# A written-out order of 3,830 pieces, replaced by another order of the same pieces

## The chip, the cores and the metric

The kernel runs on one core of a Trainium2 chip. The metric is the device time of one execution in microseconds. The core has five instruction queues that run side by side: TensorE (PE, with its weight loads PEld), VectorE (DVE), ScalarE (ACT), GpSimd (POOL) and SyncE (SP), which here issues the DMAs. Each queue runs its instructions in the order in which the program issued them; an instruction waits on semaphores for what it needs from other queues, and everything behind it on its own queue waits with it.

## The reference

32 sequences of 256 tokens with 128 channels go through one block: a layer norm and a Mamba (selective state space) layer with a residual, then a layer norm and a mixture of 8 experts, of which the router takes 2 for each token.

```python
xi, res = split(layernorm(x) @ W_in)            # 256 inner channels each
u  = silu(causal_conv4(xi) + conv_b)
dt, B, C = split(u @ W_x)                       # rank 8, 16 states, 16 states
delta = softplus(dt @ W_dt + b_dt)
h[t] = exp(delta * A) * h[t-1] + delta * u * B  # for each channel and state
y = sum_n(h * C) + u * D
x = x + (y * silu(res)) @ W_out
scores = layernorm(x) @ gate_w.T                # the best two, softmax, weights cw
x = x + sum_e cw[e] * (silu(layernorm(x) @ w1[e].T) @ w2[e].T)
```

The kernel computes all 8 experts for every token and weighs them with `cw`, which is zero for six of them.

## The kernel before

The sequences are cut into 17 tiles: tiles 0 and 16 hold one sequence, tiles 1 to 15 two. One tile goes through some 230 pieces. A piece is a small function that issues one or a few instructions, mostly to one engine. A long string, `ORDER`, lists all 3,830 pieces of all tiles as `tile:piece`, and the kernel runs through it once:

```python
    with tc.manual_schedule():
        for word in ORDER.split():
            i, n = word.split(":")
            pieces[n](int(i))
```

So the string alone sets the order within each engine's queue, and with it which buffer is given out when. No scheduler comes after it. Its words interleave about three tiles at a time: while one tile's scans run, the experts of the tile before and the convolution of the tile after stand between them. The pieces, in the order that one tile needs them, with their lines:

- Start: `ldx` (load x, SP), `st1`, `sa1` (statistics and their aggregation for the layer norm, DVE, L538 and L544), `rs1` (four small POOL instructions, L554 to L557), `ap1` (normalise, ACT, L563), `tr1`, `hi1`, `nl1`, `lo1` (transpose on PE and split into a high and a low part, PE and ACT alternately).
- Convolution: `cv0`, `cv1` (12 matmuls each, PE, L635), `u0`, `u1` (silu, ACT, L649). Gate: `gp`, `gs` (PE L703, ACT silu L718).
- State-space inputs: `wx` (PE, L658), `sb`, `rh`, `nr`, `rl` (ACT and PE), `bcd` (rows B and C to DRAM, SP), `rb`, `rc` (B and C rows broadcast to 128 partitions, SP, L778), `zz` (PE), `sp` (softplus, ACT, L739), `du` (POOL, L793), `dp` (copy of du to PSUM, ACT, L799).
- Scans, 16 for a tile of two sequences and 8 for a tile of one, 256 in all: `dk` (decays, ACT exp, L760), `in` (product du times B row into the one PSUM tile `db`, DVE, L818), `sc` (scan, DVE, L825), `cm` (weigh with the C row, POOL, L836; once `cn`, on DVE, L840), `ys` (transposing sum onto y, PE, L844; L862 for the first of a half).
- After a half of the scans: `yc` (copy y, ACT), `yz` (times gate, POOL, L924; once `yv`, on DVE), `yt` (transpose, PE), `ye` (copy, ACT, L944). Then `ldr` (x again, SP), `px` (residual, PE, L956), `op` (output matmul, PE, L966), `x2` (copy, ACT), and `st2`, `sa2`, `rs2`, `ap2`, `tr2`, `hi2`, `nl2`, `lo2` as above.
- Router: `gt` (PE), `sc` without a number (two reductions, DVE, L1052), `r0` to `r3` (DVE, L1059 to L1079), `r4`, `rw0`, `rw4`, `rw3` (POOL), `rx` (exp, ACT), `rw1`, `rw2` (DVE).
- Experts: for each of 8, `wi` twice (PE, L1125), `si` twice (silu, ACT, L1138), `wo` (16 matmuls, PE, L1146), `as` (scale by cw, ACT, L1158) and `aa` (add, POOL, L1164), or in part of the last two tiles `ad` (DVE, L1169); at the end `sto` (store, SP).

Constants are loaded and prepared by pieces of tile 0 (`lw`, `lc`, `l1`, `ld2`, `km`, `kh`, `kl`, `kw`, `pm`, `kdg`, `kgt` and others), also placed by the string.

Buffers bind the queues to one another: 9 tiles `da` of decays, 4 each of B and C rows, 3 of scan results h, one `db`, one `du`, two of x, 2 of `so` and 4 working tiles in PSUM. A scan with number k of its tile needs the h buffer that the `ys` of three scans before has freed. The B rows of four and the C rows of three scans in the middle of a tile are kept for its second half, which runs the states in the opposite order.

ACT's functions lie in three tables (exp, silu, softplus). `need()`, L530, issues a table load whenever the next function is in another table than the last one, so the number of loads follows from the order too.

Of the kernel before, what the change touches and what calls it, by code (L numbers as in the profile page):

```python
# [47 lines left out]
0:pm 0:ldx 0:lw0 0:lw1 0:lc0 0:lc1 1:ldx 0:ldp 0:st10 0:st11 0:sa1 0:rs1 0:ap1 0:km1 0:tr1 0:kh1 0:hi1 0:nl1  # L48
0:km0 0:kh0 0:lo1 0:kl1 1:st10 1:st11 1:st13 1:st12 0:kl0 0:kwr 0:cv1 0:cv0 1:sa1 1:rs1 3:ldx 3:st10 0:ldd
0:ldk 0:ka 0:u1 1:ap1 1:tr1 0:u0 0:wx 0:gp0 0:sb 0:rh 0:kdt 1:hi1 0:nr 0:rl 0:gs0 1:nl1 0:zz 0:pb0 1:lo1 0:sp0  # L50
0:pc0 0:l11 0:ldg 0:ld2 0:l10 2:ldx 2:st10 3:st13 0:kw0 0:kw1 2:st12 0:dq0 2:st11 2:st13 0:in0 2:sa1 0:bcd
0:rc0 0:rc3 0:rb1 0:rc1 0:rb2 0:dk0 0:dk2 0:dk1 0:sc0 0:cm0 0:in1 0:sc1 0:in2 0:kgt 0:sc2 0:dk5 0:dk3 2:rs1
2:ap1 0:kdg 0:cm1 1:gp0 1:cv1 1:cv0 1:u0 0:ys0 1:u1 0:dk4 0:ys1 1:wx 1:rh 1:sb 0:dk6 0:dk7 0:rb3 0:in3 0:dq1
0:sc3 0:in4 0:sc4 0:in6 0:rc7 0:rc2 0:cm2 0:cm3 0:ys2 1:nr 1:rl 0:sc6 1:bcd 0:ldr 0:ys3 1:zz 1:sp0 0:yc0 1:sp1
0:in5 3:st11 0:sc5 1:rb1 1:rb5 0:cm4 0:ys4 1:rc0 1:rb4 0:ldo 0:yz0 0:yt0 0:cm6 1:rc3 1:du0 0:cm5 0:ys5 0:px
0:ys6 0:in7 1:rb0 0:sc7 0:cm7 0:ys7 1:gp1 1:gs0 2:tr1 1:dk5 1:dp0 1:in1 1:rb6 4:ldx 3:st12 1:dk1 1:sc1 1:in0
1:dk0 1:dk3 0:ye0 1:dk8 1:dk2 0:yc1 0:yz1 2:hi1 1:rb2 1:rc1 1:sc0 1:cm0 3:sa1 0:yt1 2:nl1 0:ye1 0:op 0:st20
1:dk6 2:lo1 2:gp0 0:st21 0:sa2 0:rs2 1:cm1 1:in2 1:ys0 1:rc2 1:rb3 0:x2 1:gs1 0:ap2 0:tr2 0:hi2 1:sc2 1:in5
4:st10 1:sc5 0:nl2 0:lo2 2:gs0 0:wi50 0:gt 1:ys1 0:sc 1:in3 1:rc5 1:rc13 0:r3 1:sc3 1:cm2 1:rc4 1:rb7 0:pt
0:r4 1:cm3 1:du1 1:rc7 0:si50 1:dk9 1:dk11 1:dk4 0:rx 1:dk10 1:dk12 1:in4 2:cv1 1:ys2 0:r0 1:sc4 1:cm4 1:rc6  # L60
1:cm5 1:in6 0:r1 0:wi40 2:cv0 1:ys3 1:sc6 0:si40 0:wi70 2:u1 0:wi51 2:u0 0:wi00 0:si70 0:si51 1:in7 0:r2 2:wx
1:ys4 1:ys5 0:wi20 0:wi41 3:rs1 1:cm6 0:rw0 0:rw4 1:dk7 1:sc7 1:cm7 0:si00 0:wi21 2:rh 0:si20 0:wi60 1:dp1
1:in8 4:st13 2:sb 2:bcd 1:rb15 2:nr 0:si21 2:gp1 0:si60 0:wi01 0:si01 3:ap1 1:sc8 0:wi10 0:si10 0:si41 1:ys6
0:wi30 0:si30 2:gs1 2:rl 1:ys7 2:zz 0:wo0 3:tr1 1:in9 1:rb13 1:ldr 0:rw1 1:cm8 1:sc9 1:in10 1:rb12 0:rw2
1:sc10 0:rw3 1:in11 4:st12 1:rc11 2:rb3 2:sp0 0:wo4 2:sp1 1:yc0 3:hi1 1:ys8 1:sc11 1:in12 0:wi11 0:as4 0:wo2
0:as0 0:wi71 3:nl1 0:si11 1:dk13 3:lo1 2:dk3 1:cm9 1:rc12 1:rb14 1:ys9 1:cm10 1:ys10 3:cv0 1:yz0 0:aa4 0:as2
0:si71 1:dk15 1:dk14 1:cm11 1:ys11 0:wi61 1:rc15 4:st11 1:sc12 1:in13 2:rb0 1:rc14 4:sa1 1:sc13 1:in14 2:rb4
1:sc14 0:wo7 0:wi31 1:in15 0:aa2 0:as7 2:du0 1:cm12 2:rc0 1:ys12 1:yt0 1:cm13 0:aa0 2:du1 1:cm14 2:rb1 1:sc15
1:cm15 2:rc2 2:dk6 2:dk0 3:u0 3:gp1 1:ys13 1:ys14 1:ys15 0:si61 0:si31 2:dp0 2:in0 2:rb5 2:rc1 2:sc0 2:in1
2:rb2 2:dk7 2:dk1 2:sc1 2:in3 2:dk2 1:yc1 2:dk4 1:ye0 2:dk8 2:dk5 2:sc3 2:in2 3:cv1 3:gp0 1:px 2:rc3 2:cm0  # L70
2:ys0 2:sc2 3:u1 1:yz1 1:yt1 2:cm1 2:cm3 2:cm2 1:ye1 1:op 2:ys1 1:st20 2:in4 3:gs0 3:gs1 2:dk9 2:dk11 2:dk10
# [12 lines left out]
2:op 3:ys0 2:st20 4:tr1 3:in3 2:st21 2:st22 3:sc3 2:st23 3:in4 2:sa2 1:as4 1:wo2 3:ys1 3:sc4 3:dk7 1:as5 1:aa5
3:cm2 2:rs2 3:dk11 3:dk10 4:hi1 4:nl1 1:wo7 3:ys2 1:as2 4:lo1 2:x2 3:dk12 2:ap2 4:cv0 3:rb5 3:in5 5:sa1 3:sc5
3:rc5 3:rb7 3:rb6 3:rc4 3:rc6 2:tr2 4:u0 3:in6 6:st10 2:hi2 3:cm3 4:gp0 2:nl2 3:ys3 4:cv1 4:gs0 2:lo2 3:dk9
3:sc6 1:aa2 1:as7 3:dk13 3:cm4 5:rs1 3:du1 3:cm5 3:in7 3:dp1 3:dk15 6:st13 3:ys4 3:sc7 3:cm6 3:rc12 3:rc7 2:gt
2:sc 3:in8 2:r0 3:rb13 3:ys5 2:wi00 4:gp1 2:si00 2:wi30 4:u1 4:wx 4:gs1 2:wi60 3:ys6 3:sc8 3:cm7 5:ap1 2:si60
2:si30 4:sb 2:r1 3:in9 2:r3 3:sc9 3:ys7 2:wi20 2:si20 4:rh 2:wi70 2:wi61 4:nr 2:si70 3:yc0 4:rl 2:si61 3:dk14
3:in10 2:r2 3:sc10 2:wi50 3:cm8 3:ys8 3:cm9 3:ys9 4:zz 2:wi21 1:aa4 2:r4 2:rx 2:rw0 3:ldr 3:rc13 3:rb12 4:bcd  # L90
3:rc11 4:rb1 3:in11 4:sp0 2:wi71 4:sp1 2:wi31 2:si21 2:si31 2:si71 2:rw4 2:rw1 3:sc11 3:in12 3:cm10 3:ys10
2:wi01 5:tr1 2:wi40 2:si01 2:si50 2:si40 2:wi10 2:si10 5:hi1 2:wi41 2:wi51 2:rw2 3:sc12 4:du0 1:aa7 3:cm11
3:cm12 2:rw3 3:yz0 3:rb14 3:rc15 3:in13 3:rb15 3:rc14 4:rb4 3:sc13 3:in14 3:cm13 4:rb0 2:wi11 2:si11 2:si51
2:si41 3:ys11 2:wo2 2:wo3 3:ys12 5:nl1 3:yt0 3:sc14 4:rc0 4:rc1 3:cm14 4:dk3 4:dk2 2:as3 2:as2 2:aa3 3:ys13
2:wo1 3:ys14 2:wo0 3:in15 4:dp0 6:st11 4:rb3 3:sc15 4:in0 6:st12 3:cm15 4:rb2 2:aa2 3:ys15 4:dk0 4:sc0 4:cm0
# [12 lines left out]
4:in15 7:st11 4:rc14 4:cm14 5:rb4 4:rc15 5:rb0 5:rb3 5:dp0 6:lo1 5:dk7 4:ys13 3:aa1 3:wo5 4:ys14 3:wo0 5:dk4
3:as5 3:as2 4:sc15 4:cm15 3:aa5 4:ys15 3:wo4 4:yc1 3:as0 4:yz1 5:dk2 5:in1 5:rc0 5:rb2 7:st12 5:sc1 5:in0
# [1162 lines left out]
```

## Time and profile before

| | us |
|---|---|
| Median of 3 runs (lowest, highest) | 1044.05 (1043.04, 1046.95) |
| The profiled execution | 1043.46 |
| Its span, first to last instruction | 1041.7 |
| POOL weighing `cm` L836, 255 instructions | 604.2 busy, 2.38 each |
| DVE scan L825, 256 | 584.3 busy, 2.28 each |
| DVE product L818, 256 | 314.9 busy, 1.23 each |
| ACT decays L760, 544 | 341.1 busy |
| ACT table loads L530, 105 | 134.7 busy, 1.28 each |
| PE sums `ys` L844, 2,048 matmuls | 268.8 busy |
| PE expert matmuls L1125 and L1146 | 215.8 and 249.1 busy |
| Landing of a C row (median), 205 loads of 512 KB | 5.1 |
| Landing of a B row (median), 187 loads of 512 KB | 4.8 |

The span is what lies between the first and the last instruction. An engine's busy time leaves out its waits. A wait is named by the engine that waits and the work that released it. Matmuls are pipelined, so a mean duration of a matmul is longer than its share of PE's time.

### The profile page before, as it was taken

To read this page: it belongs to the slowest core of one execution; us is meant where nothing else is said; L and a number is where in the kernel's file an instruction comes from. 1 tells how busy PE (TensorE), PEld (TensorE's weight loads), DVE (VectorE), ACT (ScalarE), POOL (GpSimd) and SP (SyncE) were. 2 spreads that over 40 slices of the span, in tenths; PEclk is the share of its full clock that TensorE was granted. 3 is DMA by queue.
4 is the path that set the end of the run, shared out by engine and by line. 5 is a ranking of instruction groups with operands and counts; after the bars stand their busy time and mean duration, and the time that the engine had idled before them with its cause. 6 is when DMAs were issued, how large, how long until landed. Compare 5 with 4: busy or idle time off the path is not lost.

```text
span 1041.7 us, 18833 instructions
## 1 busy us (share of the span) xinstructions
PE 952.9 (91%) x6693; PEld 833.6 (80%) x6693; DVE 967.1 (93%) x946; ACT 944.7 (91%) x1893; POOL 901.8 (87%) x676
## 2 busy tenths in 40 slices
PE   6578789899999999999999999999989999899998
PEld 5467678879798888879888887888878788787888
DVE  4999999999999999999999999999999999999963
ACT  6889989989899999989999898989979999899975
POOL 2668888999899999998899999998989999899962
PEclk9789999999999999999999999999999999999999
DMA  7474848668476776847586685858668585865500
GB/s 234 155 258 161 284 167 274 219 215 284 172 256 189 254 257 205 282 157 260 197 266 240 209 268 174 273 175 277 222 196 272 179 279 178 269 232 197 182 11 16
DMA packets 86094, 223.75 MB, mean 215 GB/s; under 512 B 8048, under 2 KB 35312, under 8 KB 85872
## 3 DMA queue, kind: packets, MB, share of 16 engines
q1 hardware_dynamic: 86000, 222.55, 64.5%
q8 instruction: 52, 0.85, 0.3%
q14 instruction: 42, 0.34, 0.1%
HBM read 217.28 MB, written 5.24 MB: 214 GB/s over the span
## 4 chain that ended last, share of the span: by engine, by line
PE 31%; ACT 26%; DVE 21%; POOL 15%; issue 6%; DMA 1%; SPq 0%; DVEq 0%; POOLq 0%; ACTq 0%
DVE h L825 13%; ACT da L760 9%; PE pf L1125 9%; POOL h L836 9%; PE pe L1146 7%; DVE db L818 6%; PE y L844 6%; ACT L530 5%; POOL x L1164 3%; ACT so L1158 3%; PE pc L635 3%; ACT hs L1138 2%; PE po L966 1%; PE pd L658 1%; ACT xn_c L563 1%
## 5 line engine op out<-in xcount | busy, mean ns | idle before, releaser
L836 POOL TENSOR_TENSOR h<-h,rc 128x1024 f32<-128x1024 f32 x255 | 604.2, 2379 | 67.4 <-DVE h L825 56.3
L825 DVE TENSOR_TENSOR_SCAN h<-da,db 128x1024 f32<-128x1024 f32 x256 | 584.3, 2282 | 21.9 <-PE y L844 7.6
L760 ACT ACTIVATE da<-de,a_sb 128x510 f32<-128x510 f32 (+1 forms) x544 | 341.1, 718 | 0.9 <-DVE h L825 0.5
L818 DVE TENSOR_TENSOR db<-du,rb 128x1024 f32<-128x1024 f32 x256 | 314.9, 1230 | 11.2 <-ACT du L799 2.1
L844 PE MATMUL y<-ident,h 128*128 128x128 f32 x2048 | 268.8, 278 | 20.0 <-POOL h L836 19.5
L844 PEld LDWEIGHTS y<-ident,h 128*128 128x128 f32 x2048 | 237.2, 144 | 39.2 <-POOL h L836 26.7
L1146 PE MATMUL pe<-w_sb,hs 128*128 128x128 f32 x2048 | 249.1, 276 | 3.8 <-ACT so L1158 2.8
L1146 PEld LDWEIGHTS pe<-w_sb,hs 128*128 128x128 f32 x2048 | 238.8, 192 | 11.3 <-ACT so L1158 4.4
L1125 PE MATMUL pf<-xt,w_r 128*128 128x512 f32 (+1 forms) x816 | 215.8, 399 | 12.5 <-ACT hs L1138 7.3
L1138 ACT ACTIVATE hs<-pf 128x512 f32<-128x512 f32 (+1 forms) x272 | 144.6, 577 | 40.3 <-PE pf L1125 36.6
L1125 PEld LDWEIGHTS pf<-xt,w_r 128*128 128x128 f32 x816 | 138.6, 189 | 52.9 <-ACT hs L1138 19.7
L1164 POOL TENSOR_TENSOR x<-x,so 128x512 f32<-128x512 f32 (+1 forms) x126 | 157.5, 1250 | 10.5 <-ACT so L1158 9.2
L1158 ACT ACTIVATE so<-pe,cw 128x128 f32<-128x128 f32 x488 | 140.4, 393 | 6.4 <-PE pe L1146 4.1
L530 ACT ACT_TABLE_LOAD x105 | 134.7, 1283 | 1.9
L635 PE MATMUL pc<-xt_r,wc_r 128*128 128x512 f32 (+1 forms) x408 | 99.9, 396 | 1.1 <-ACT xt_r L624 1.1
L635 PEld LDWEIGHTS pc<-xt_r,wc_r 128*128 128x128 f32 x408 | 73.8, 197 | 15.4 <-issue 0.8
L862 PE MATMUL y<-dg_sb,u 128*128 128x128 f32 x256 | 36.4, 285 | 11.7 <-ACT yt L917 6.9
L862 PEld LDWEIGHTS y<-dg_sb,u 128*128 128x128 f32 x256 | 32.6, 195 | 17.0 <-ACT yt L917 10.6
L924 POOL TENSOR_TENSOR g<-yt,g 128x512 f32<-128x512 f32 (+1 forms) x33 | 40.7, 1233 | 5.6 <-ACT yt L917 2.9
L793 POOL TENSOR_TENSOR dus<-de,u 128x512 f32<-128x512 f32 (+1 forms) x32 | 39.8, 1247 | 0.0
L966 PE MATMUL po<-wo_sb,yt 128*128 128x128 f32 x256 | 32.8, 277 | 2.3 <-ACT yt L944 2.2
L966 PEld LDWEIGHTS po<-wo_sb,yt 128*128 128x128 f32 x256 | 30.8, 192 | 4.9 <-ACT yt L944 3.2
(101 smaller groups left out, 716.8 us busy)
## 6 DMA issues: line engine op xcount, KB each, us to landing
rc<-bc SPq DMA_DIRECT2D x205, 512.0 KB, 5.1
rb<-bc SPq DMA_DIRECT2D x187, 512.0 KB, 4.8
xa<-in_x SPq DMA_DIRECT2D x15, 256.0 KB, 4.4
xc<-in_x SPq DMA_DIRECT2D x15, 256.0 KB, 4.4
out<-x SPq DMA_DIRECT2D x15, 256.0 KB, 6.0
w1h<-in_w_t SPq DMA_DIRECT2D x2, 512.0 KB, 7.1
w_sb<-in_w_t SPq DMA_DIRECT2D x1, 1024.0 KB, 7.6
bc<-s SPq DMA_DIRECT2D x32, 32.0 KB, 3.1
```

What stands on the lines that cost most here:

```text
L530: nc.scalar.preload_act_table_set(SETS[which])
L635: nc.tensor.matmul(pcv, wc_r[a][:, j, c * P : (c + 1) * P], xt1_r[b][:, : nb[i], o + j : o + j + L], start=(k == 0), stop=(k == 3 * KC - 1),)
L760: nc.scalar.activation(da[:, m, :, 1:], de[:, :, 1:], AF.Exp, scale=a_sb[:, c, n : n + 1])
L818: nc.vector.tensor_mul(db, d["du"].unsqueeze(1).to_broadcast([P, gs[i], tok[i]]), rows["b", i, k])
L825: nc.vector.tensor_tensor_scan(flat(h), da_of(i, k), flat(d["db"]), 0.0, ALU.mult, ALU.add,)
L836: nc.gpsimd.tensor_tensor(h, h, rows["c", i, k], ALU.mult)
L844: nc.tensor.matmul(y[:, q, :], src[:, q * P : (q + 1) * P], ident, is_transpose=True, start=False, stop=last, skip_group_check=True,)
L1125: nc.tensor.matmul(pf, w1_r[a][:, e, f * P : (f + 1) * P], d["xt"][b], start=(k == 0), stop=(k == 2),)
L1138: nc.scalar.activation(d["hs", e][:, f, :], d["pf", e, f], AF.Silu)
L1146: nc.tensor.matmul(pe[:, q, :], hs[:, f, q * P : (q + 1) * P], w2_sb[:, e, f, :], start=(f == 0), stop=(f == FC - 1),)
L1158: nc.scalar.activation(so[:, q, :], d["pe", e][:, q, :], AF.Copy, scale=d["cw"][:, q, e : e + 1])
L1164: nc.gpsimd.tensor_tensor(x2, x2, st[i]["so", e], ALU.add)
```

## The change

Nothing but the string `ORDER` is replaced, on lines 47 to 284. Both strings hold the same 3,830 words. 3,627 of them stand at another place; a word is moved by 10.1 places on average and by 187 at most, and the longest run of words that keep their order among themselves has 1,769. The arithmetic, the buffers and the number of instructions that the pieces issue stay as they are. The number of table loads that follows from the order is 105 before (106 with the first one, L563) and 106 after (107).

The first lines of both, and the words from the last scan on:

```diff
-0:pm 0:ldx 0:lw0 0:lw1 0:lc0 0:lc1 1:ldx 0:ldp 0:st10 0:st11 0:sa1 0:rs1 0:ap1 0:km1 0:tr1 0:kh1 0:hi1 0:nl1
-0:km0 0:kh0 0:lo1 0:kl1 1:st10 1:st11 1:st13 1:st12 0:kl0 0:kwr 0:cv1 0:cv0 1:sa1 1:rs1 3:ldx 3:st10 0:ldd
-0:ldk 0:ka 0:u1 1:ap1 1:tr1 0:u0 0:wx 0:gp0 0:sb 0:rh 0:kdt 1:hi1 0:nr 0:rl 0:gs0 1:nl1 0:zz 0:pb0 1:lo1 0:sp0
...
-16:sc7 16:cn7 15:rw1 15:rw2 15:rw3 16:yz0 14:aa4 14:sto 15:wo5 16:px 15:wo1 16:ys5 16:ys6 15:si01 16:yt0 16:ys7
-16:yv1 15:as1 15:wi21 16:ye0 16:yt1 15:as5 15:wi61 16:ye1 16:op 16:st20 16:st21 16:sa2 16:x2 15:si61 15:si21
...
+0:ldx 0:lw0 0:lc0 0:lc1 0:ldg 1:ldx 0:ldk 0:ldd 0:ldp 0:l11 0:lw1 0:l10 0:ld2 0:st10 0:st11 0:sa1 0:pm 0:rs1
+0:ap1 3:ldx 0:km1 0:tr1 0:kh1 0:hi1 0:nl1 0:lo1 1:st10 1:st13 1:st12 0:kl1 0:cv1 1:st11 1:sa1 1:rs1 0:kdg 0:km0
+0:ka 0:kh0 1:ap1 2:ldx 0:u1 0:kwr 0:kl0 0:cv0 1:tr1 0:u0 0:wx 0:gp0 0:rh 0:sb 1:hi1 0:nr 0:rl 0:gs0 0:kdt 0:zz
...
+16:sc7 15:rw1 16:cn7 16:ys7 16:yt0 15:wi21 16:yv1 15:wo1 15:rw2 15:rw3 15:as5 15:si21 16:ye0 16:px 16:yt1 15:wi61
+16:ye1 15:as1 15:si61 15:aa1 16:op 16:st20 16:st21 16:sa2 16:x2 16:rs2 15:wo0 15:as0 16:ap2 15:wo3 15:wi71 16:tr2
```

The line breaks are set anew here. ACT's decays from the end of tile 13 to the start of tile 14, in the order in which they are issued (other words between them left out):

```diff
-13:dk10 13:dk8 13:dk11 13:dk9 13:dk12 13:dk15 13:dk13 13:dk14 14:dk0 14:dk1 14:dk2 14:dk3 14:dk4 14:dk5 14:dk6
+13:dk12 13:dk8 13:dk11 13:dk10 13:dk9 13:dk15 13:dk13 13:dk14 14:dk0 14:dk3 14:dk1 14:dk4 14:dk5 14:dk2 14:dk6
```

## The prediction

> **What bounds the kernel now.** I read the page first, then busy time by stretches, then the waits, then VectorE's own timeline. The page and the stretches:
>
> ```profile
> span 1041.7 us, 18833 instructions
> PE 952.9 (91%) x6693; PEld 833.6 (80%) x6693; DVE 967.1 (93%) x946; ACT 944.7 (91%) x1893; POOL 901.8 (87%) x676
> ...
> 0.00:60.00 60.00, 35.35 (x162) 29.03 (x163) 45.87 (x58) 47.52 (x88) 28.75 (x46) 0.83 0.59 199
> 190.00:320.00 130.00, 125.35 (x906) 111.10 (x904) 125.73 (x124) 123.55 (x248) 120.88 (x88) 1.00 0.69 227
> 960.00:1042.00 82.00, 76.09 (x599) 71.08 (x597) 52.56 (x78) 61.27 (x152) 51.83 (x45) 1.00 0.23 81
> ```
>
> The columns of a stretch are its length and the busy time of PE, PE's weight loads, DVE, ACT and POOL. In the middle four engines are busy over 90% of the time and DVE most, 125.73 of 130. At the end PE leads and DVE has little left. So the middle is VectorE's, and the end TensorE's.
>
> ```profile
> 122.22 1.23 DVE L818 TENSOR_TENSOR db<-du,rb 128x1024 f32<-128x1024 f32 x1
> 123.59 2.29 DVE L825 TENSOR_TENSOR_SCAN h<-da,db 128x1024 f32<-128x1024 f32 x1
> 125.91 1.23 DVE L818 TENSOR_TENSOR db<-du,rb 128x1024 f32<-128x1024 f32 x1
> 127.28 2.29 DVE L825 TENSOR_TENSOR_SCAN h<-da,db 128x1024 f32<-128x1024 f32 x1
> ...
> 235.56 1.23 DVE L818 TENSOR_TENSOR db<-du,rb 128x1024 f32<-128x1024 f32 x1
> 236.70 0.28 DVE L538 BATCH_NORM_STATS2 st_a<-xa 128x6 f32<-128x128 f32 x1
> 236.92 2.29 DVE L825 TENSOR_TENSOR_SCAN h<-da,db 128x1024 f32<-128x1024 f32 x1
> ```
>
> This is VectorE's timeline (start, duration). With nothing else between, scan follows scan after 3.69 us (127.28 - 123.59), and product to scan takes 1.37. With a 0.28 us statistic between product and scan it takes 1.36 (236.92 - 235.56): the small piece runs in a gap that is there anyway.
>
> That lets me write the span as a sum. The first scan starts at 25.92 and the last at 1002.96. Between them lie 255 intervals; 255 x 3.69 = 941.0, and 1002.96 - 25.92 = 977.0, so 36.1 us are lost in the middle. In VectorE's timeline the idle times in brackets between these two scans add up to 16.7 us (36 waits, none over 1.2); the other 19.4 are small pieces that found no gap. Head 25.9 + 941.0 + 36.1 + end 38.7 = 1041.7. The profiled execution took 1043.46, 1.8 more than its span, and the median is 1044.05, 0.6 above that; I subtract from the median.
>
> ```profile
> DVE h L825 <- PE y L844: 7.6, 14, 1.2
> POOL h L836 <- DVE h L825: 56.3, 46, 13.5
> POOL h L836 <- DMA rc<-bc: 5.8, 3, 4.6
> ```
>
> The waits (total, times, longest): the scan mostly waits for the transposing sums `ys`, which free one of the three h buffers. The rest of the 16.7 is ACT's du copy 2.1, router scores from PE 1.8, `po` 1.5, decays `da` 1.3 and single cases.
>
> **The change, part by part.** No instruction is added or taken away but one activation-table load. Every saving must come from the head, the 36.1 or the end.
>
> *The 941.0 stays:* the same 256 scans and products, both orders with one product in each interval.
>
> *Small pieces on VectorE.* I sorted the 255 intervals by what the order puts between two scans, and before (pre) or after (mid) the product, and priced each pattern by its undisturbed intervals in the timeline, as the excess over 3.69: one statistic mid 0.02, four aggregates mid 0.06, `r0` mid 0.11, `st in st` 0.05, `st in st st` 0.25, `r0 in r1` 0.29, `r1 in r2` 0.29. The old order then costs 20.5 (19.4 by the subtraction above), the new one 18.5. The difference, 2.0, is mostly these: `st in st st` goes from 6 intervals to 0 (-1.5) while `st in st` goes from 3 to 10 (+0.4), `r0 in r1` from 4 to 2 (-0.6) while `r1 in r2` goes from 4 to 6 (+0.6), and two long router and statistics clusters, of tiles 16 and 1, lose 0.3 each. I take -2.0; bounds -3 and 0.
>
> The Trainium skill ("VectorE: DVE Perf Modes", section "The DRAIN you can't avoid") says that the next op starts only when the pipe is empty, and advises to minimize the number of ops. By that rule a small piece costs the same wherever it stands, and this term would be 0. The rows above speak against it: 0.28 us of statistic between product and scan cost nothing.
>
> *Waits of VectorE, 16.7.* What makes `ys` late is other work crowded in front of it on PE, or POOL's weighing `cm` behind other work. h has three buffers, so I looked at three scans at a time: the row times of all that stands in an engine's queue between one `ys` (or `cm`) and the third after it, less 3 x 3.77 (3.77 is 977.0 less 16.7, over 255). Row times are 0.9 for a `ys`, 1.8 for a `wo`, 0.75 for a `wi`, 2.8 for a `cv`, 2.38 for a `cm`, 1.28 for an `aa`. On PE the worst stretch exceeds by 10.5 in the old order and by 7.5 in the new; over all stretches the excess is about the same (+3%). On POOL the worst falls from 8.2 to 6.7, the sum by 21%. A wait arises only where a stretch outruns the buffers, so I go by the worst ones: 7.5 / 10.5 = 0.71, and 16.7 x 0.71 = 11.9, or -4.8. Bounds: -16.7 (all gone) and +16.7 (an equal amount of new ones, since nearly every queue is reshuffled).
>
> *Loads on SP.* I counted for each row load how many scans lie between the one that frees its buffer and the one that needs it. C rows with a lead of one scan: 3 in the old order, 0 in the new; leads of two: 19 and 17; B rows are as before (1 and 1, 35 and 36). Their cover is the lead: two scans are 7.4 us, against a median landing of 5.1. POOL waited only 5.8 us for such rows, and VectorE hardly felt it, so 0; without that cover a late C row costs up to the 4.6 of its longest wait. `ldr` moves forward by 26 places on average, past row loads; it needs a freed x buffer, and a blocked SP would delay the rows behind it. I keep that inside the +16.7.
>
> *The table load.* The order alternates exp, silu and softplus 105 times before, 106 times now. One load is 1.28 us of ACT, which in the middle idles 6.4 of 130 us, and its lead over VectorE covers it: 0. Uncovered it costs 1.3, since ACT's queue then delays a decay and VectorE's next scan.
>
> ```profile
> 961.56 1.28 ACT L530 ACT_TABLE_LOAD   x1
> 962.86 2.56 ACT L760 ACTIVATE da<-de,a_sb 128x510 f32<-128x510 f32 x4
> ```
>
> The skill ("ScalarE: Activation LUTs", section "What ACT_TABLE_LOAD costs") puts a switch at 2.66 us, 1.28 of load and 1.38 of drain, which would make it 2.7. Here the exponential starts 1.30 us after the load began, so the trace has the load alone.
>
> *The head.* Convolution weights are issued one place earlier (0.47 us, half of 0.93 for two w_in issues), `rh` now stands before `sb` (0.46), and the dg_sb diagonals no longer come late, for which PE sat 4.9 us without holding up a scan. But ACT has the same work queued between `wx` and the first decay, some 8.7 us from 17.2 to 25.9, and the first silu still waits for an exp table, four normalisations and a silu table. I take 0; bounds -0.9 and +1.3 (a table load uncovered).
>
> *The end.* After `16:sc7` the last `ys` started 3.9 us after its scan ended; weighing and a 0.18 us sum need 1.4 of that, the rest was PE's queue. In the new order `15:wo1` (1.95), `16:px` (0.60) and `16:yt0` (0.38) stand behind that `ys` instead of before it: 2.5 come free ahead of it, 2.9 are added behind. I take 0; bounds -2.4 and +2.9.
>
> Sum: -2.0 - 4.8 + 0 + 0 + 0 = -6.8. 1044.05 - 6.8 = 1037.2, or 0.65% faster.
>
> **Rivals.** *The waits only change places.* If every crowded stretch that is thinned has a new one elsewhere, only VectorE's packing is left: 1044.05 - 2.0 = 1042.1, no change that a measurement of this kernel can tell (I count 0.5%, 5.2 us). For it: PE's excess summed over all stretches is the same. Against it: on both engines the worst stretches shrink, and POOL's sum too. Its own range is 1038.9 to 1049.2.
>
> *Late decays between tiles 13 and 14.* From the decay of `13:sc12` to that of `14:sc2` ACT's queue exceeds VectorE's pace by 36.3 us in the new order (row times scaled to the 944.7 of busy ACT), where the worst stretch before was 27.4. Nine da buffers give at most 9 x 3.77 = 33.9 of lead, so some 2.4 us of wait appear if ACT is fully ahead, and 36.3 - 27.4 = 8.9 if it is no further ahead than it ever had to be. The price is then 8.9 - 2.0 = +6.9: 1051.0, slower. It decides from a wait of 7.2 us, with no gain elsewhere. For it: `14:dk2` now stands behind `14:dk4` and `14:dk5`. Against it: VectorE waited only 1.3 us for decays, and the long stretch begins with a decay issued early, nine scans ahead.
>
> *That the order does not reach the engines* is excluded: the built queues of PE, ACT, DVE, POOL and SP all differ.
>
> **How the numbers follow.** Forecast (waits shrink) 0.50; waits change places 0.36; slower, by late decays or a like convoy, 0.14. These are also the chances of faster, within and slower by 0.5%. The low end: -2.0, -12 of the 16.7 and -2.4 at the end make 1027.7, so 1028. The high end takes in most of the no-change case: 2.0 gained, some 6 of new waits, 1048. About 0.06 lies below, 0.14 above. As both signs have weight, the forecast's own range is 1028 to 1038.8.
>
> **What would show it.** The first scan at 25 to 27 us; 3.69 between bare scans; idle time of VectorE between first and last scan near 12 instead of 16.7, with `PE y` the main releaser and near 5; small pieces about 17 to 18.5; from the last scan's start to the end 38 to 39. I am wrong in the packing if `st in st st` cost nothing to lose; in the waits if their sum is 16 or more; and in the mechanism if the head or the end moves by more than 3 us, or if `da` or `rc` becomes the main releaser.

## The result: 0.44% slower, and the profile after

The new order took 1049.86 us (median of 20 runs, 1045.96 to 1052.68), the old one beside it 1044.70 (20 runs, 1042.70 to 1048.36). The ratio is 1.0044, interval 1.0032 to 1.0055: slower for certain, though by less than the 0.5% that I counted as a change. The forecast was 1037.2; the time lies outside the range, above its 1048.

The page after, with the lines that answer to those shown of before:

```profile
span 1051.0 us, 18854 instructions
...
PE 961.5 (91%) x6693; PEld 839.4 (80%) x6693; DVE 968.8 (92%) x946; ACT 946.4 (90%) x1894; POOL 903.0 (86%) x676
...
PEclk9869999999999999999999999999999999999999
```

The profiled execution took 1052.68, the longest of its runs, while that of before (1043.46) was among the shorter of its own. So the two spans lie 9.3 us apart where the times differ by 0.44%, some 4.6 us: about half of what the two profiles show against each other is the draw of these executions. Instructions and busy times are as before (VectorE 968.8 against 967.1). What grew is idle time. The last row is TensorE's granted clock in tenths, in 40 slices; the second and third are at 0.8 and 0.6 (before 0.7 and 0.8).

The waits after (total, times, longest):

```profile
POOL h L837 <- DVE h L826: 65.0, 51, 17.8
...
DVE h L826 <- PE y L845: 9.9, 14, 2.2
DVE db L819 <- ACT du L800: 5.4, 10, 1.2
...
POOL h L837 <- DMA rc<-bc: 1.9, 4, 1.1
```

The scan's waits for the sums rose from 7.6 to 9.9, where I had expected near 5; those for `du` from 2.1 to 5.4. C rows are waited for less than before (1.9 against 5.8).

I cut both profiled spans as the prediction did: time up to the first scan, then for each tile the excess over 3.69 us per scan (the time between two scan starts is counted to the tile of the later one), then the stretch from the last scan's start. Tile 16 and the end are taken together.

| us | first scan | tile 0 | 1 | 2 | 3 | 4 to 14 | 15 | 16 and end | span |
|---|---|---|---|---|---|---|---|---|---|
| old order | 25.9 | 3.3 | 2.0 | 0.6 | 2.1 | 21.9 | 1.9 | 43.0 | 1041.7 |
| new order | 28.3 | 3.7 | 5.7 | 3.2 | 2.8 | 19.2 | 3.9 | 43.1 | 1051.0 |

So in these two executions the new order is better by 2.7 us over the eleven tiles in the middle, and worse by 9.8 in the first 250 us: 2.4 + 0.4 + 3.7 + 2.6 + 0.7. Tile 15 costs another 2.0. The tables of the experiments below use the same columns.

What happened at the start can be read from the granted clock. A stretch's row gives its length, the busy time of PE, PE's weight loads, DVE, ACT and POOL, and then the granted clock. Before:

```profile
20.00:30.00 10.00, 7.97 (x37) 6.08 (x35) 8.98 (x15) 9.95 (x20) 1.71 (x1) 1.00 0.96 350
70.00:85.00 15.00, 13.49 (x81) 10.51 (x81) 14.83 (x15) 14.11 (x24) 11.24 (x9) 1.00 0.58 189
```

After:

```profile
20.00:30.00 10.00, 9.48 (x29) 7.21 (x30) 6.17 (x12) 9.12 (x18) 0.00 (x0) 0.66 0.81 258
70.00:85.00 15.00, 12.48 (x53) 10.59 (x53) 13.04 (x14) 10.77 (x20) 12.39 (x14) 0.66 0.62 203
```

Two stretches that ran at full clock now run at 0.66 on average. The clock record has only two values here, 1.0 and 0.5: in the new order 0.5 was granted from 21.9 to 28.8 us, 42.4 to 49.2, 52.7 to 62.9, 73.1 to 83.4, 155.1 to 158.5 and 926.5 to 929.9. That is 41.0 us. The old order had 27.3 us: 20.5 between 32.7 and 60.0, where PE has little to do, and 3.4 each at 118 and at 470.

In the head the chain of waits runs through the eight `pb` matmuls that spread B and C of tile 0. PE's timeline before, then after (start, duration, and in brackets the idle time and what ended it):

```profile
19.58 1.88 PE L882 MATMUL pb<-s,ident 64*128 64x256 f32 x8
```

```profile
13.80 2.07 PE L636 MATMUL pc<-xt_r,wc_r 128*128 128x256 f32 x8 [0.73 <-DVE wc_r L486]
21.37 3.25 PE L883 MATMUL pb<-s,ident 64*128 64x256 f32 x8
```

They started 1.8 us later and took 1.4 us longer. Two things stand behind the later start: `0:cv0` waited 0.73 us for its weights, since VectorE had `0:kwr` queued ahead of `0:kl0` and stood 2.63 us for the transfer that `0:kwr` needs; and the four `pd` matmuls behind it took 1.97 us instead of 1.08. ScalarE then waited 0.83 for `pb`, and the first decay and scan came 2.4 us later.

The experiments show that these 2.4 us belong to this one execution and not to the order. e2, e9 and e13 below have the new order's words, unaltered, up to the first scan, and there it starts at 26.2, 25.3 and 25.8 us; with the old order's words it starts at 25.9 to 26.5 in ten traces. In these three `0:cv0` has no such wait, and VectorE stands 1.4 to 1.7 us for that transfer instead of 2.63. The first record of full clock also comes at 18.5 us in this execution, and at 12.1 to 16.0 in all the other seventeen traces; the `pd` matmuls at 16.7 us ran ahead of it.

### The profile page after: what moved, and what is told of

Read it like the earlier page. It is cut to its first block, busy times and chain, and to the rows that moved or that the text cites. A ratio compares the mean times of both kernels' runs of the same rounds, so it can differ in the third digit from the quotient of the medians.

```text
span 1051.0 us, 18854 instructions
## 1 busy us (share of the span) xinstructions
PE 961.5 (91%) x6693; PEld 839.4 (80%) x6693; DVE 968.8 (92%) x946; ACT 946.4 (90%) x1894; POOL 903.0 (86%) x676
## 4 chain that ended last, share of the span: by engine, by line
PE 31%; ACT 31%; DVE 18%; POOL 11%; issue 8%; DMA 1%; SPq 0%; DVEq 0%; POOLq 0%; ACTq 0%
DVE h L826 11%; PE pf L1126 11%; ACT da L761 10%; POOL h L837 6%; ACT L531 6%; PE y L845 6%; DVE db L819 6%; PE pe L1147 5%; ACT so L1159 4%; ACT hs L1139 4%; PE pc L636 2%; POOL x L1165 2%; PE po L967 1%; PE pg L704 1%; ACT de L740 1%
## 5 line engine op out<-in xcount | busy, mean ns | idle before, releaser
L1159 ACT ACTIVATE so<-pe,cw 128x128 f32<-128x128 f32 x488 | 140.1, 394 | 10.1 <-POOL cw L1118 4.4
L636 PE MATMUL pc<-xt_r,wc_r 128*128 128x512 f32 (+1 forms) x408 | 102.2, 403 | 1.4 <-DVE wc_r L486 0.7
L580 PE MATMUL pyt<-ident,g 128*128 128x128 f32 x128 | 20.9, 285 | 14.1 <-POOL g L925 12.4
```

The costliest lines, as they stand in the source:

```text
L636: nc.tensor.matmul(pcv, wc_r[a][:, j, c * P : (c + 1) * P], xt1_r[b][:, : nb[i], o + j : o + j + L], start=(k == 0), stop=(k == 3 * KC - 1),)
L1159: nc.scalar.activation(so[:, q, :], d["pe", e][:, q, :], AF.Copy, scale=d["cw"][:, q, e : e + 1])
```

## The experiments

Two theories are set against each other. T1: the loss lies in the first 170 us, where TensorE stands still, is granted half clock for it, and then delays sums and scores. T2: the loss is in the order of the late tiles and the end, or spread over the whole of it. "Old up to w, then new" means: all words that the old order has before w, then all others in the new order. Every kernel was timed beside the kernel before, with 5 to 12 runs of its own; the columns from the first scan on come from one profiled execution each. The figures stand here together:

| kernel | median us | ratio, interval | first scan | tile 0 | 1 | 2 | 3 | 4 to 14 | 15 | 16 and end | span |
|---|---|---|---|---|---|---|---|---|---|---|---|
| e1 old up to `2:sc0`, then new | 1047.37 | 1.0022, 1.0010 to 1.0035 | 26.0 | 3.3 | 3.7 | 5.0 | 2.8 | 19.1 | 4.0 | 43.1 | 1047.9 |
| e2 new up to `2:sc0`, then old | 1052.11 | 1.0066, 1.0048 to 1.0085 | 26.2 | 3.7 | 5.8 | 5.4 | 3.9 | 20.4 | 1.9 | 43.0 | 1051.4 |
| e3 `0:kl0` earlier | 1048.89 | 1.0040, 1.0026 to 1.0053 | 25.6 | 3.7 | 4.5 | 3.3 | 2.8 | 19.3 | 3.9 | 43.1 | 1047.1 |
| e4 dummy matmuls | 1049.81 | 1.0052, 1.0034 to 1.0069 | 26.3 | 3.7 | 2.0 | 5.8 | 2.8 | 19.3 | 3.9 | 43.1 | 1047.8 |
| e5 old up to `4:sc0`, then new | 1045.11 | 1.0008, 0.9992 to 1.0023 | 26.0 | 3.3 | 2.3 | 0.6 | 3.4 | 20.6 | 2.3 | 43.1 | 1042.6 |
| e6 as e5, old from `15:sc0` | 1051.88 | 1.0074, 1.0055 to 1.0093 | 26.1 | 3.3 | 2.3 | 0.7 | 3.4 | 20.1 | 10.6 | 43.0 | 1050.3 |
| e7 e1, `3:zz` behind `1:r4` | 1047.28 | 1.0029, 1.0019 to 1.0039 | 26.3 | 3.3 | 2.3 | 4.2 | 2.8 | 19.1 | 3.9 | 43.1 | 1045.9 |
| e8 e3, e4 and e7's move | 1051.27 | 1.0059, 1.0039 to 1.0079 | 26.7 | 3.7 | 2.3 | 7.0 | 2.8 | 19.0 | 3.9 | 43.1 | 1049.7 |
| e9 new, `3:zz` behind `1:r2` | 1053.35 | 1.0080, 1.0064 to 1.0097 | 25.3 | 3.7 | 4.3 | 11.1 | 2.0 | 20.8 | 3.9 | 43.1 | 1055.1 |
| e10 e1, `3:zz` behind `1:r2` | 1051.74 | 1.0055, 1.0041 to 1.0069 | 26.3 | 3.3 | 2.3 | 7.9 | 2.0 | 20.7 | 3.9 | 43.1 | 1050.5 |
| e11 old up to `7:sc0`, then new | 1044.97 | 1.0000, 0.9987 to 1.0012 | 26.1 | 3.3 | 2.0 | 0.7 | 2.1 | 21.0 | 2.3 | 43.1 | 1041.8 |
| e12 e1, two `wi` later | 1045.50 | 1.0003, 0.9990 to 1.0016 | 26.1 | 3.3 | 2.3 | 0.8 | 2.8 | 19.1 | 2.3 | 43.1 | 1040.6 |
| e13 new, two `wi` later | 1047.96 | 1.0021, 1.0009 to 1.0034 | 25.8 | 3.7 | 4.5 | 3.2 | 2.8 | 19.0 | 2.3 | 43.1 | 1045.3 |
| e14 e13, e3 and e4 | 1047.95 | 1.0021, 1.0006 to 1.0036 | 26.0 | 3.7 | 2.0 | 2.2 | 2.8 | 19.0 | 3.9 | 43.1 | 1043.6 |
| e15 e12, old from `16:sc6` | 1045.25 | 0.9999, 0.9984 to 1.0015 | 26.5 | 3.3 | 2.0 | 0.9 | 2.8 | 19.1 | 2.3 | 42.9 | 1040.8 |
| e16 old, new from `5:sc0`, old from `16:sc6` | 1043.18 | 0.9989, 0.9972 to 1.0006 | 26.5 | 3.3 | 2.3 | 0.6 | 3.4 | 18.2 | 4.0 | 44.2 | 1043.4 |

**Where the loss is: e1, e2, e5, e11.** The start of one order before the rest of the other.

```diff
 (e1) ORDER = old words before 2:sc0 + the others in the new order
 (e2) ORDER = new words before 2:sc0 + the others in the old order
```

> The old order's first 387 words (up to 2:sc0), then the new order for all other words. Theory 1 (the loss sits in the first 100 us, where PE gaps let the granted clock fall to a half; the rest of the new order is better packed): first scan near 25.9 us, excess over 3.69 us per interval in tiles 0 to 2 near 6 us as before instead of 12.6, tiles 4 to 14 near 19 us as in the changed kernel, time 1042 to 1045 us. Theory 2 (the profiled start of the changed kernel was one bad draw, and the loss sits in tile 15 and the end, +3.5 us): time 1048 to 1050 us.

> The new order's first 382 words (up to 2:sc0), then the old order for all other words. Theory 1: the loss comes along whole: first scan near 28 us, time 1049 to 1053 us. Theory 2: time 1043 to 1046 us.

e2's time came as T1 has it, but its first scan at 26.2 and not near 28, and it is slower than the whole new order: tiles 2 and 3, where its two orders join, cost 5.4 and 3.9. e1 fell between the two: half of the loss was left, and its tile 2 (5.0) is worse than in the new order itself. So the cut had to go behind tile 2.

```diff
 (e5)  ORDER = old words before 4:sc0 + the others in the new order
 (e11) ORDER = old words before 7:sc0 + the others in the new order
```

> The old order up to the first scan of tile 4, the new order for all that is left. If the loss lies in the start (T1): head and tiles 0 to 3 as before (25.9 us to the first scan, excess over 3.69 us per scan 8.0 us), tiles 4 to 14 as in the new order (19 us, before 22), tile 15 near 3.9, tile 16 near 2.9 and the end near 40.2, so a span near 1041 and a time within 1.5 us of the kernel before. If the loss lies in the late tiles and the end, or is spread over the order (T2): 1046 or more, as most of the 16 ratios of tiles 4 to 16 would have to be worse.

> The old order up to the first scan of tile 7, the new one for the rest. By the tiles of the earlier traces: head and tiles 0 to 6 as before (13.4 us of excess), tiles 7 to 14 as in the new order (12.5, before 17.4), tile 15 between 2.3 and 3.9, tile 16 at 2.9, the end at 40.2: a span of 1039 to 1040, 1.5 to 2.5 below that before, and some 1 us back if the join costs, as it did at tile 4. T1 forecasts 1041 to 1043, ratio 0.997 to 0.999. If the new order's middle is worth nothing without its own start: 1044 or more.

With the old order up to tile 4 most of the loss is gone: 1.0008, an interval that takes in 1 but reaches 1.0023. The late tiles and the end are the new order's there, so the loss lies ahead of them; e11 at 1.0000, and below e12 at 1.0003 with the new order from `2:sc0` on but for two words, say the same. From the ratios, 0.22% (2.3 us) of the 0.44% belongs to the words before `2:sc0`, 0.14% to those between `2:sc0` and `4:sc0`, and 0.08% to the rest, each with an error of nearly 0.2%. The shares need not add up: e2, with its join, has 0.66% with the same words before `2:sc0`. e11 lay at the old order's time, 2 us above what its tiles promised: a miss on the gain.

**What makes the start slow, first try: e3 and e4, in the new order.**

```diff
 (e3)
-0:kwr 0:kl0 0:cv0
+0:kl0 0:kwr 0:cv0
 (e4) in psw, ahead of the use of seven PSUM tiles of tiles 0 to 2
+    HOT = {"pd_0": 4, "pg_0_0": 4, "pz_0_0": 4, "po_0": 6, "pg_2_0": 4, "pt_c0": 6, "pf_0_5_1": 4}
+    for _ in range(HOT.get(name, 0)):
+        nc.tensor.matmul(t[:, :P], ident, ident, start=True, stop=True, ...)
```

> The new order with one word moved: 0:kl0 stands before 0:kwr, so that the second convolution half of tile 0 no longer waits behind a VectorE copy that waits for the late half of w_in (PE waited 0.73 us in the middle of it). Theory 1, in the form that this gap starts the loss: first scan 1 to 2.4 us earlier, clock 1.00 up to 26 us, time 1046 to 1048 us. Theory 1, in the form that the many other gaps of the start do it: first scan up to 1 us earlier, time 1048.5 to 1050 us. Theory 2: no change, 1049 to 1051 us.

> The new order, with 32 additional 128x128 matmuls of the identity with itself, written into working tiles of tiles 0 to 2 just before these are filled (4 to 6 each before wx, gp0, zz, px, tr2 and one wi of tile 0 and gp0 of tile 2), which only fill PE's gaps; some 4 us of PE work more. Theory 1: the mean granted clock of the runs rises from 0.978 to 0.985 to 0.985 or more, time 1045 to 1049 us in spite of more work. Theory 2: no gain, 1050 to 1053 us.

The trace counts the dummies as 64 more matmuls (6,757 against 6,693); the 256 that a later expectation names is a slip of mine. In e3 the first scan came at 25.6, before the old order's 25.9, but the median hardly moved (1.0040). As e2, e9 and e13 reach 25.3 to 26.2 without the moved word, e3 had little or nothing to mend. e4 answers about tile 1. The same stretch and the same matmuls in e4:

```profile
70.00:85.00 15.00, 12.64 (x83) 10.86 (x82) 14.70 (x15) 13.76 (x24) 13.03 (x10) 1.00 0.60 206
```

```profile
72.35 1.31 PE L1131 MATMUL pf<-xt,w_r 128*128 128x256 f32 x9
...
74.59 1.97 PE L850 MATMUL y<-ident,h 128*128 128x128 f32 x16
```

and in the new order without the dummies:

```profile
74.37 2.29 PE L1126 MATMUL pf<-xt,w_r 128*128 128x256 f32 x9 [0.46 <-ACT xt L1022]
...
78.01 3.67 PE L845 MATMUL y<-ident,h 128*128 128x128 f32 x16
```

Nine `wi` matmuls take 1.31 us instead of 2.29 and sixteen sums 1.97 instead of 3.67. What the slow ones cost VectorE in the new order:

```profile
78.19 0.19 DVE L1053 TENSOR_REDUCE sc<-psc 128x16 f32<-128x32 f32 x1 [1.51 <-PE psc L1038]
...
80.07 2.29 DVE L826 TENSOR_TENSOR_SCAN h<-da,db 128x1024 f32<-128x1024 f32 x1 [0.39 <-PE y L845]
...
89.41 2.29 DVE L826 TENSOR_TENSOR_SCAN h<-da,db 128x1024 f32<-128x1024 f32 x1 [1.89 <-PE y L845]
```

It stood 1.51 us for the router's scores, 0.39 and 1.89 for sums; in e4 none of the three waits is there, and tile 1 costs 2.0 as in the old order. So tile 1's loss is the half clock. All eighteen traces agree with that. Without half clock between 68 and 84 us tile 1 costs 2.0 to 2.3 (six traces), with one stretch of 3.4 us 2.3 (six), with 6.8 us 3.7 to 4.5 (four), with 10.2 us 5.7 or 5.8 (two). The five traces that have the new order's start and no dummies had 6.8 or 10.2 us of it there; of the ten with the old start only e1 had 6.8, the others 3.4 or none. The order makes this half clock likely, and the execution decides how much of it comes.

e4 was not faster for it, as tile 2 then lost 5.8; and e4's runs had the higher mean clock (0.987 against 0.982). Half clock in sum is therefore not the whole cause: it matters where it falls, and something else delays tile 2.

**Tile 2: e7 to e10, and e12, e13.** PE's and then VectorE's timeline of e1:

```profile
163.58 0.40 PE L712 MATMUL pz<-rh,wdt_r 128*128 128x256 f32 x2
167.21 0.79 PE L712 MATMUL pz<-rh,wdt_r 128*128 128x256 f32 x2 [3.24 <-DVE rank L1058]
167.81 1.91 PE L828 MATMUL y<-ident,h 128*128 128x128 f32 x8
...
170.79 3.19 PE L828 MATMUL y<-ident,h 128*128 128x128 f32 x16
```

```profile
166.74 0.41 DVE L1058 TENSOR_REDUCE rank<-psc 128x32 f32<-128x256 f32 x1
169.81 2.29 DVE L809 TENSOR_TENSOR_SCAN h<-da,db 128x1024 f32<-128x1024 f32 x1 [2.65 <-PE y L828]
```

The second `pz` of `3:zz` stands 3.24 us until VectorE has done the rank of `1:r2`: it has been given the one of the four `ps_w` buffers that the router's scores hold until then. Behind it in PE's queue stand the sums `2:ys9` to `2:ys11`; after the stand they run at half clock (eight in 1.91 us), and the scan `2:sc12` waits 2.65 us. In the new order's own profile the same stand is 1.56 us, no half clock follows it, and `2:sc12` waits 1.52 us; tile 2 costs 3.2 there (PE's and VectorE's timeline):

```profile
172.31 0.51 PE L729 MATMUL pz<-rh,wdt_r 128*128 128x256 f32 x2 [1.56 <-DVE rank L1075]
```

```profile
173.78 2.29 DVE L826 TENSOR_TENSOR_SCAN h<-da,db 128x1024 f32<-128x1024 f32 x1 [1.52 <-PE y L845]
```

In the old order `3:zz` stands ahead of `2:ys8`, and it was `1:wi60` that got the buffer: a stand of 1.11 us, behind `2:ys9`, after which no scan of tile 2 waits. PE's timeline of before:

```profile
164.94 0.96 PE L1125 MATMUL pf<-xt,w_r 128*128 128x512 f32 x3 [1.11 <-DVE rank L1074]
```

I first moved `3:zz` behind the wrong word:

```diff
 (e7, in e1; e8, in the new order with e3's and e4's edits)
-... 3:zz 3:sp0 3:sp1 2:rc12 2:in12 1:r4 ...
+... 2:rc12 2:in12 1:r4 3:zz 3:sp0 3:sp1 ...
```

> The kernel with the old start and the new rest, and in it three words moved: 3:zz, 3:sp0 and 3:sp1 stand behind 1:r4 (the rank that sets free the fourth PSUM buffer) instead of before it. If tile 2 lost its time because TensorE stood 3.2 us for that buffer and then ran at half clock (T1): the wait of pz on rank is gone, there is no half-clock stretch at 166 us, the excess of tile 2 falls from 5.0 to between 1.5 and 3, and the time from 1047.4 to about 1044.5. If the half clock comes anyway (T2): tile 2 stays at 4 to 6 and the time at 1047.

> The new order with three things mended: the weight load of 0:kl0 before 0:kwr, the dummy matmuls of the earlier run (256 of 128x128, which add TensorE work and nothing else), and 3:zz, 3:sp0, 3:sp1 behind 1:r4. If the loss of the start is TensorE's waits and the half clock after them (T1): first scan at 25.6 to 26.3 us, tiles 0 to 2 together near 8 to 9 us of excess (15.0 in the new order's profile, 5.9 before), span near 1044 and a ratio near 1.002. If the loss is in the order of the start for another reason (T2): tile 1 or 2 stays above 4 and the ratio at 1.004 or more.

Both missed: `1:r4` does not release the buffer, and the stand stayed (3.00 and 3.22 us). Then behind the right one:

```diff
 (e9, in the new order; e10, in e1)
-... 3:zz 3:sp0 3:sp1 ... 3:du0 1:r2 ...
+... 1:r2 3:zz 3:sp0 3:sp1 3:du0 ...
```

> The new order with four words moved: 3:zz, 3:sp0, 3:sp1 and 3:du0 behind 1:r2. The run before with a like move (behind 1:r4) changed too little: the second pz still took the PSUM bank that the router's scores hold until the rank of 1:r2. Now it is 1:wi21 that takes this bank, and it stands behind the sums 2:ys9 to 2:ys11. T1 (TensorE's stand at that bank is what delays the sums of tile 2): no wait of pz on rank, the excess of tile 2 from 3.2 in the new order's profile to between 0.6 and 2, the median lower by 2 to 4 us, some 1046 to 1048. T2 (half clock alone): tile 2 stays at 3 or more and the median at 1049 to 1050.

> The same four words moved in the kernel with the old start (up to the first scan of tile 2) and the new rest. There tile 2 had an excess of 5.0 us against 0.6 in the old order. T1: the wait of pz on rank (3.2 us) is gone, no half clock at 166 us, tile 2 at 0.6 to 2, and the median from 1047.4 to some 1044 (ratio 0.999 to 1.001). T2: tile 2 at 4 or more, 1047.

The stand was gone and the sum was in time, but both kernels were slower. ScalarE's and VectorE's timelines of e10 show the price:

```profile
168.88 0.60 ACT L723 ACTIVATE de<-pz 128x512 f32<-128x512 f32 x1 [4.95 <-PE pz L712]
...
171.98 1.33 ACT L744 ACTIVATE da<-de,a_sb 128x510 f32<-128x510 f32 x2
173.22 0.21 ACT L1076 ACTIVATE ex<-ex 128x32 f32<-128x32 f32 x1
```

```profile
173.86 0.19 DVE L1092 TENSOR_REDUCE sm<-cw 128x4 f32<-128x32 f32 x1 [4.29 <-POOL cw L1087]
```

Its softplus of `pz` now stood 4.95 us, the router's exponential `ex` behind it, POOL's weights behind that, and VectorE stood 4.29 us for them. So I left `3:zz` where it is and changed who gets the buffer:

```diff
 (e12, in e1; e13, in the new order)
-... 1:wi61 1:wi31 1:wi41 ... 3:zz ... 2:ys9 1:wi01 ... 2:ys10 2:cm11 2:ys11 1:wi21 ...
+... 1:wi61 1:wi31 ... 3:zz ... 2:ys9 ... 2:ys10 2:cm11 2:ys11 1:wi41 1:wi01 1:wi21 ...
```

> The kernel with the old start up to 2:sc0 and the new rest, and in it 1:wi41 and 1:wi01 moved behind 2:ys11; 3:zz and its softplus stay where they are, so that ScalarE's order is untouched. Now 1:wi41 takes the PSUM bank that the router's scores hold, and it stands behind the sums. If TensorE's stand of 3.2 us at that bank is what costs tile 2 its time (T1): no such wait before the sums 2:ys9 to 2:ys11, no half clock at 166 us, 2:sc12 without a wait, tile 2 from 5.0 to between 0.6 and 2.5, the median from 1047.4 to some 1044 to 1045. If tile 2 is slow for another reason (T2): 4 or more, 1047.

> The same two words moved in the whole new order. T1: tile 2 from 3.2 (in the new order's profile) to between 0.6 and 2.5, the median from 1049.9 to some 1047 to 1048; the late head and tile 1 stay. T2: 1049 to 1050.

PE and VectorE in e12:

```profile
161.43 0.66 PE L712 MATMUL pz<-rh,wdt_r 128*128 128x256 f32 x4
161.93 1.91 PE L828 MATMUL y<-ident,h 128*128 128x128 f32 x16
166.06 1.09 PE L828 MATMUL y<-ident,h 128*128 128x128 f32 x8 [2.23 <-POOL h L820]
```

```profile
164.95 0.42 DVE L1058 TENSOR_REDUCE rank<-psc 128x32 f32<-128x256 f32 x1
165.28 2.28 DVE L809 TENSOR_TENSOR_SCAN h<-da,db 128x1024 f32<-128x1024 f32 x1
```

Four `pz` in 0.66 us without a stand, sixteen sums in the 1.91 us that eight took in e1, and `2:sc12` follows the rank without a wait. Tile 2 falls from 5.0 to 0.8. The ratio goes from 1.0022 to 1.0003, and in the new order from 1.0044 to 1.0021; in each pair the intervals still overlap a little, but two pairs and the traces agree on some 2 us, of the 4.6 lost, for this one buffer. In e13's profile tile 2 kept 3.2: a stretch of half clock at 170.6 and a wait of 1.78 for a sum at `2:sc15`.

**The three edits together: e14.**

```diff
 (the new order)
-0:kwr 0:kl0 0:cv0
+0:kl0 0:kwr 0:cv0
+the dummy matmuls of e4
+1:wi41 1:wi01 behind 2:ys11
```

> The new order with the three places of its start mended together: 0:kl0 before 0:kwr (first scan near 25.6 to 26.3 us), the dummy matmuls of the earlier run (tile 1 at 2.0 to 2.3), and 1:wi41 and 1:wi01 behind 2:ys11 (tile 2 at 0.6 to 2.5). T1: head and tiles 0 to 2 within 3 us of the old order's, span 1043 to 1044, time 1044.5 to 1046.5 and a ratio of 1.000 to 1.002. T2 (the start costs by something else): 1048 or more.

Its profile is as T1 has it, clock 1.0 from 60 us up to tile 15, tiles 1 and 2 at 2.0 and 2.2; its median is not: 1047.95, no better than e13. The twelve runs spread from 1043.57 to 1051.62 and only one of them is traced. Their granted clock is on record, and time goes with it: the two fastest (1043.57 and 1044.11) had a mean of 0.993, the slowest 0.985, the correlation is -0.92. So the slower runs drew more half clock; where it fell in them isn't known. The dummies are work of their own, so this isn't a fair price of the half clock, and why the median stays 0.21% above the old order's though its mean clock is higher (0.990 against 0.984) stays open.

**The late part, and a better mixture: e6, e15, e16.**

```diff
 (e6)  ORDER = old before 4:sc0, new before 15:sc0, old
 (e15) ORDER = e12's before 16:sc6, old
 (e16) ORDER = old before 5:sc0, new before 16:sc6, old
```

> The old order up to the first scan of tile 4, the new one for tiles 4 to 14, the old one from the first scan of tile 15. If the pieces add up as the tiles of the earlier traces say (T1): as before but 2.8 us less in tiles 4 to 14, so 1041 to 1042 and a ratio near 0.997, the end at 38.8 and tile 15 near 1.9. If the new middle only pays because of the start that stood before it, or if the joins cost (T2): 1044 or more.

> The kernel with the old start up to 2:sc0, 1:wi41 and 1:wi01 moved and the new rest, but with the old order again from 16:sc6 on, where no word that the old order had done is still missing. The new end lasted 40.2 us from the last scan's start in every profile with it, the old one 38.8. If that difference belongs to the words behind 16:sc6: end at 38.8, all else as in the run before with a span of 1040.6, so 1.4 us less, a ratio near 0.999. If it is brought about by what stands before 16:sc6: end at 40.2 and a ratio of 1.000.

> The old order up to 5:sc0, the new one up to 16:sc6, the old one again behind it: both cuts where at most five words are out of step. By the tiles: head 25.95, tiles 0 to 4 9.9 us of excess, tiles 5 to 14 16.6 (before 20.1), tile 15 2.3, tile 16 2.9, end 38.8: a span of 1037.4 against 1041.7, a ratio near 0.996 if the half clock is drawn alike; 0.999 to 1.000 if the cuts cost 3 us or more, as one at 15:sc0 did (8.7).

e6 failed at its second join: tile 15 cost 10.6, with waits of 2.55, 1.87 and 1.93 for sums and `po` where words of both orders pile up. In e15 the old words from `16:sc6` on brought the end back to 38.8 us, but tile 16 from 2.9 to 4.2: together 42.9 against 43.1. The longer end of the new order is work moved from tile 16, and costs nothing. e16 has the lowest median of all, 1043.18, with a ratio of 0.9989 (0.9972 to 1.0006): not told apart from the old order (in its profile half clock at 919 and 943 us cost tiles 15 and 16 some 3 us), and no version was found that beats it for certain.

**What tile 15 lost.** The same words there cost 3.9 in most of these kernels and 2.3 in e5, e11, e12, e13 and e15. PE's timeline in the new order, then in e12:

```profile
926.40 1.09 PE L580 MATMUL pyt<-ident,g 128*128 128x128 f32 x4 [2.78 <-POOL g L925]
927.29 3.19 PE L1147 MATMUL pe<-w_sb,hs 128*128 128x128 f32 x16
```

```profile
917.69 0.66 PE L563 MATMUL pyt<-ident,g 128*128 128x128 f32 x4 [2.78 <-POOL g L908]
918.18 1.95 PE L1130 MATMUL pe<-w_sb,hs 128*128 128x128 f32 x16
```

Both stand 2.78 us for POOL's `g`. Only in the first did half clock follow (926.5 to 929.9), and sixteen `wo` matmuls took 3.19 us instead of 1.95. All five traces with 2.3 are without half clock there, and all ten with 3.9 or 4.0 have a stretch of 3.4 us that begins between 919 and 931 us. The stand is the order's, the 1.6 us are the clock's.

## Why the prediction was wrong, step by step

*The 941.0 stays*: right; undisturbed scans still follow each other after 3.69 us.

*Small pieces, -2.0*: measured 0.0 (19.4 before and after, by the same subtraction). The named patterns did what they were priced at: `st in st st` -1.65 for the -1.5, `st in st` +0.45 for the +0.4, `r0 in r1` -0.55, `r1 in r2` +0.77. But I summed the patterns that I had named: `st st in st` (+0.7), statistics with four aggregates (+0.6) and bare products a little off 3.69 (+0.55) took it back. The price list was right, the sum over it incomplete. The page that the prediction sets against its rows, the Trainium skill's "VectorE: DVE Perf Modes", says in the same section ("The DRAIN you can't avoid") that a next op that isn't held starts earlier, so page and rows need not contradict each other.

*Waits, -4.8*: the step that failed. I put 16.7 to 11.9 and found 22.1 (21.3 in the traces of e3 and e4, which leave nearly all of the order as it is). By tiles the scaling held where it was made for: tiles 4 to 14 went from 11.5 to 8.7, a factor of 0.76 against my 0.71; whether the ratio of the worst stretches is a sound rule or came near by luck, one pair of orders can't tell. Tiles 0 to 3 went from 2.0 to 9.5, and 15 and 16 from 3.3 to 3.9. I judged the crowding of PE's queue by row times of the middle. In the start these rows don't hold: sixteen sums take 3.67 us there instead of 1.97, and a `pz` that no row of PE's crowd makes late waits for a buffer that VectorE frees. The page of before had the clock at 0.7 and 0.8 in two of its first slices, and I did not make a term of it. Nor did I ask, for a moved piece, which PSUM buffer it would be given.

*Loads, table load*: 0 was right; C rows are waited for less (1.9 against 5.8).

*The head, 0*: +2.4 in the one profile, outside my bounds of -0.9 to +1.3 (they had a table load in them and no slower matmul). But with the same words up to the first scan e2, e9 and e13 have +0.3, -0.7 and -0.1: for the order the 0 held, and the 2.4 are the draw of one execution.

*The end, 0*: +1.5, inside the bounds, and paid for by tile 16 (-1.3), as e15 shows.

Of the rivals, "the waits only change places" came nearest: waits fell in the middle and rose at the start. But it had them even out and gave 1042.1, up to 1049.2 at most; they rose by more than they fell. The late decays did not come: VectorE waited once in all for a decay, 1.5 us at the very first scan, and tile 14 cost 1.4 against 0.9. The prediction's own test, wrong in the waits if their sum is 16 or more, has decided: 22.1.

Of the 0.44% (4.6 us), then, about half was placed before `2:sc0` (above all the half clock in tile 1), and some 2 us in tile 2 (the buffer, shown by moving two words); the rest is within the error. Tile 0 costs 0.4 more and tile 3 0.7 more with the new order's words; what makes them so was not traced. e3's median could hardly fall, since its head was not late. In e4's profile tile 2 lost what tile 1 gained, with a stand of 3.21 us for the buffer and half clock after it; whether its other runs did the same isn't known.

## What to carry to other kernels

Price a new order stage by stage, with each stage's own row times: the fill of the pipeline has other rows than the middle, and a list tuned in the middle can lose there what it gains. When a piece is moved, ask also which rotating buffer it will now be given and who frees it; a matmul that waits for a buffer stops all that is queued behind it. And where a stand of TensorE is long, ask whether slower matmuls after it add to its price. When two profiles are set against each other, look first where each stands among the runs of its kernel: here half of their difference was the draw, and with it all of the 2.4 us in the head.

## What the runs showed of the hardware

*TensorE can lose the full clock without standing still for a whole window.* All stretches of half clock last multiples of 3.41 us, but for those that the end of a trace cuts off. I laid a grid of 3.41 us through each of the eighteen traces, in phase with its stretches, and took PE's busy share (by its modelled ends) in each window at full clock between 10 and 1033 us. All 62 windows that were busy below 40% were followed by a window at half clock; of those at 40 to 50% 20 of 42, at 50 to 60% 10 of 75, above that 17 of some 5,000. The Trainium skill ("TensorE: Matmul & The Clock Gate", section "What's actually happening") says that the window is about 3.4 us and free-running, and that the clock falls after at least one idle window. The lengths agree, and so does the free-running grid: the same stand of 2.78 us was followed by half clock in one kernel and not in another. That the window must be idle does not agree: of the 109 windows that half clock followed, PE stood still throughout in only 11, and the measurement decides.

*The spread of this kernel's runs is mostly that draw.* Over the 120 runs of the old order that stood beside the experiments, time and mean granted clock go together with a correlation of -0.76, -3.9 us for each 0.01 of clock; over the 20 runs of the new one with -0.74 and -5.2. The mean clock differs by 0.0016 (0.9839 and 0.9823), which by these slopes answers for 0.6 to 0.9 of the 4.6 us; at a clock of 0.985 the fitted lines lie at 1044.3 and 1048.1. So how much half clock there is explains little of the loss; what runs in it, and the buffer, weigh more.
